# Four weight tiles per run of products in layer 3, and layer 2's scales computed one residual later, in a four-layer graph network on one core

## The chip, the cores and the metric

The kernel runs on one core of a Trainium2 chip. The metric is the device time of one execution in microseconds (us). Before the change it was 2642.23 us, the median of three runs (2640.15 to 2648.64). The profiled execution, from which every duration below comes, took 2647.62 us; its span in the trace is 2645.6 us.

## The reference, cut to what matters

Sixteen graphs of N = 1024 nodes with D = 256 features go through four layers. Each layer adds its result to the stream `x`:

```python
h = jnp.maximum(_layernorm(x), 0.0); x = x + L0(h, adj)   # attention, softmax over the column
h = jnp.maximum(_layernorm(x), 0.0); x = x + L1(h, adj)   # attention, softmax over the row
h = jnp.maximum(_layernorm(x), 0.0); x = x + L2(h, adj)   # mean over the neighbours, relu
h = jnp.maximum(_layernorm(x), 0.0); x = x + L3(h, adj)   # attention with 4 heads of 64, norm per head
```

What the change touches is two steps. Layer 3's attended sum is `einsum('bhij,bhje->bhie', attention, h)` for each of four heads. Layer 2's mean divides by the number of neighbours, `deg`; the kernel folds `deg` into the scale of the layer norm ahead of layer 2, and that scale needs the standard deviation of rows that layer 1 has just written.

## The kernel before, in words

**Tiling.** A graph's nodes are NT = 8 tiles of 128. A "weight tile" `p` is 128 x 1024: 128 neighbours j against all 1024 nodes i. VectorE makes each with one instruction (L920 in layer 3, L812 in layer 1, L759 and L761 in layer 0), and TensorE takes 128-column pieces of it as stationary operand. In layers 0 and 1 a product is 128x128 against 256 or 257 columns (L749, L805) and a graph has 64 of them. In layer 3 there are 4 heads x 8 tiles = 32 weight tiles a graph, and each is used for 8 pieces of nodes, each piece cut in two halves of 64 columns so that the two halves lie in different columns of the array (L930): 16 products a tile, 512 a graph. Every fp32 product leaves two records in the trace, so a weight tile of layer 3 is 32 records.

**Runs.** Layer 3 gives out its weight tiles in runs of `run`: `run` instructions L920 first, and then all their products as one block. `run` is 2, and 1 for the last graph. In a block the last tile's two first pieces stand first (one for each of the two accumulators), then the earlier tiles, then the rest of the last. So a block begins when its last tile is there, and the first tile of a block is released after 4 + 16 of the block's products. The tiles come from a ring of five buffers (tag `p3`, L919): a sixth tile waits until the first has been used. The two accumulators of a head (`ps_o3`, L915) are emptied by ScalarE at the head's end (L938, twice), and the next head's products use the same two.

**The order of the work.** Each graph is a generator that yields a planned time after each piece; L1037 to L1045 always advance the one with the earliest due time. Graphs start 120 units apart while one takes about twice that, so layers 0 and 1 of one graph lie among layers 2, 3 and the tail of the one before. A scheduler then sets the order on each engine from these priorities and its own estimate of readiness; only what is wrapped in `later` keeps program order. [...]

**The norm ahead of layer 2.** `residual` (L719) is called for each node tile i: VectorE adds e and v to x (L726, L727), and after every odd i calls `Norm.pair`: VectorE makes the shifts (L638), ScalarE squares two tiles for their variances (L643). After i = 3 and i = 7, `stds` has GpSimd make the inverse deviations of four tiles (L592, then the power L593). In the norm ahead of layer 2 alone (`times` is given), `stds` then has VectorE make the scales at once (L621, L622), which wait for GpSimd; then `pair` has ScalarE make the normalised tiles hn (L659) for two pairs, TensorE transpose them (`flip`, L672) and ScalarE copy them out (L673).

**Layer 1's sums** are in a ring of two accumulators (`at_ps`): the products of tile i + 2 wait until ScalarE has read those of tile i twice (L828, L830), and these wait for a reciprocal on VectorE (L826).

**Also concerned:** the tail of the graph before (L953 to L990: VectorE, with two squares on ScalarE, L964, whose results use the ring of five too), and the masks of the graph after (L575 on ScalarE, each fed by a load L566).

Of the kernel before, what the change touches and what calls it, by code (L numbers as in the profile page):

```python
# [11 lines left out]
OP = mybir.AluOpType  # L12
# [409 lines left out]
def tile_simple_stack(  # L422
# [11 lines left out]
    nc = tc.nc  # L434
    B, N, D = x.shape
    NT = N // P
# [111 lines left out]
    class Mask:  # L548
# [4 lines left out]
        def __init__(self, b):  # L553
            self.b, self.next, self.raws = b, 0, []
            self.bytes = None
            for _ in range(self.AHEAD):
                self.load()
# [38 lines left out]
    def new_ht():  # L596
        return state.tile([P, DC, N], F32, tag="ht", name="ht", bufs=2)

    class Norm:
# [4 lines left out]


        def __init__(self, times=None):
            self.ht, self.rs, self.waiting, self.times = new_ht(), [], None, times
            if times is not None:
                self.shifts = small.tile([P, NT], F32, tag="shifts", name="shifts", bufs=2)
                self.scales = small.tile([P, 2, NT], F32, tag="scales", name="scales", bufs=2)  # L610
            self.mv = small.tile([P, NT, 2], F32, tag="mv", name="mv", bufs=4)
            self.mean, self.var = self.mv[:, :, 0], self.mv[:, :, 1]

        def stds(self, n, scale):

            k = len(self.rs)
            rs = inv_std(self.var[:, k : k + n], n, scale, 1e-5)
            self.rs += [rs[:, i : i + 1] for i in range(n)]
            if self.times is not None:
                part = slice(k, k + n)  # L620
                nc.vector.tensor_tensor(self.scales[:, 0, part], rs[:, :n], self.times[:, part], op=OP.mult)  # L621
                nc.vector.tensor_tensor(self.scales[:, 1, part], self.scales[:, 0, part], self.shifts[:, part], op=OP.mult)  # L622

        def pair(self, xs, g, sums=None):

            if self.times is None:
                self.flip()
                shift = small.tile([P, 2], F32, tag="shift", name="shift")
            else:
                shift = self.shifts[:, 2 * g : 2 * g + 2]  # L630
            if sums is None:
                for k in range(2 * g, 2 * g + 2):
                    st = small.tile([P, 6], F32, tag="bn", name="st")
                    nc.vector.bn_stats(st, xs[:, k, :])
                    nc.vector.bn_aggr(self.mv[:, k, :], st)
                nc.vector.tensor_scalar(shift, self.mean[:, 2 * g : 2 * g + 2], -1.0, None, op0=OP.mult)
            else:
                nc.vector.tensor_scalar(shift, sums, -1.0 / D, None, op0=OP.mult)  # L638
            if self.times is None:
                self.shifted(xs, g, [(1.0, shift[:, k : k + 1]) for k in range(2)])  # L640
            if sums is not None:
                for k in range(2):
                    nc.scalar.activation(  # L643
                        unread, xs[:, 2 * g + k, :], AF.Square, bias=shift[:, k : k + 1], accum_out=self.var[:, 2 * g + k : 2 * g + k + 1]
                    )
            if sums is None and g == NT // 2 - 1:
                self.stds(NT, 1.0)
            elif sums is not None and g % 2:
                self.stds(NT // 2, 1.0 / D)
                if self.times is not None:  # L650
                    for gg in (g - 1, g):
                        self.flip()
                        self.shifted(xs, gg, [[self.scales[:, k, n : n + 1] for k in range(2)] for n in (2 * gg, 2 * gg + 1)])

        def shifted(self, xs, g, by):
            hns = []
# [24 lines left out]
    def new_hs(name="hs"):  # L681
        return state.tile([P, NT, W3], F32, tag="hs", name=name, bufs=3)
# [36 lines left out]
    def residual(xs, i, v, after, e=None):  # L719

        x = xs[:, i, :]
        if i % 2 == 0:
            after.flip()
            after.sums = small.tile([P, 2], F32, tag="sums", name="sums")
        if e is not None:
            nc.vector.scalar_tensor_tensor(x, e, 1.0, x, op0=OP.min, op1=OP.add)  # L726
        nc.vector.scalar_tensor_tensor(x, v, 0.0, x, op0=OP.max, op1=OP.add, accum_out=after.sums[:, i % 2 : i % 2 + 1])  # L727
        if i % 2:
            after.pair(xs, i // 2, after.sums)
# [159 lines left out]
    def layer3(b, xs, mask, norm, res):  # L889
        hs = new_hs()  # L890
        terms = hs[:, :, D:]
        run = 2 if b < B - 1 else 1
        hb = new_hs("hb")
        hbv = hb[:, :, : H * HW].rearrange("p t (h e) -> p t h e", e=HW)
        for n in range(NT):
            ps = project(norm, wx[3], n, W3)
            nc.scalar.activation(hs[:, n, :], ps[:, :W3], AF.Copy, scale=norm.rs[n])
            if n % 2:
                pair = slice(n - 1, n + 1)
                nc.scalar.activation(hbv[:, pair, :, HO], terms[:, pair, H:], AF.Exp, scale=S3)  # L900
                t = hbv[:, pair, :, :HO]
                hv = hs[:, pair, :D].rearrange("p t (h e) -> p t h e", e=HO)
                bias = rows["bias3"].rearrange("p (h e) -> p h e", e=HO).unsqueeze(1).to_broadcast([P, 2, H, HO])
                nc.vector.tensor_tensor(t, hv, bias, op=OP.add)
                nc.vector.tensor_tensor(t, t, hbv[:, pair, :, HO:].to_broadcast([P, 2, H, HO]), op=OP.mult)
            yield 1.15
        d_row = spread(column(terms[:, :, :H], H), H, (S3 - 1.0,), "l3")
        row = everywhere(d_row[0], "row3")
        watch(b, 2, terms)
        q = small.tile([P, NT, H], F32, tag="q3", name="q3", bufs=2)  # L910
        nc.scalar.activation(q, terms[:, :, H:], AF.Exp, scale=1.0 - S3)
        yield 9.44
        for h in range(H):
            next_row = everywhere(d_row[h + 1], "row3") if h + 1 < H else None
            pss = [hd_ps.tile([P, HALF], F32, tag="hd", name="ps_o3") for _ in range(NHALF)]  # L915
            for j in range(0, NT, run):
                ps_ = []
                for jj in range(j, j + run):
                    p = work.tile([P, N], F32, tag="p3", name="p3", bufs=5)  # L919
                    nc.vector.scalar_tensor_tensor(p, row, q[:, jj, h : h + 1], mask[:, jj, :], op0=OP.max, op1=OP.mult)  # L920
                    ps_.append(p)


                last = run - 1
                runs = [(last, 0), (last, PER)] + [(t, i) for t in range(run) for i in range(NT) if t < last or i % PER]
                for t, i in runs:
                    g, k = divmod(i, PER)
                    for c in range(2):
                        part = slice(c * P // 2, (c + 1) * P // 2)
                        nc.tensor.matmul(  # L930
                            pss[g][part, k * HW : (k + 1) * HW], ps_[t][:, i * P : (i + 1) * P][:, part], hbv[:, j + t, h, :],
                            start=(j == 0 and t == last and k == 0), stop=(j == NT - run and t == last and k == PER - 1),
                            skip_group_check=True,
                        )
                yield 1.4 * run
            for g in range(NHALF):
                o = pss[g][:, : PER * HW].rearrange("p (k e) -> p k e", e=HW)
                nc.scalar.activation(res[:, g * PER : (g + 1) * PER, h, :], o, AF.Relu)  # L938
            row = next_row
        return hs  # L940
# [53 lines left out]
    def graph(b):  # L994
        xs = loaded.pop(b)
        m = masks.pop(b)
        norm = Norm()
        for g in range(NT // 2):
            norm.pair(xs, g)
            m.step()  # L1000
            yield 2.66
        for layer, inputs in ((layer0, (m,)), (layer1, (m.bytes,)), (layer2, ())):
            yield 2.36
            norm.flip()
            after = Norm(degrees(b) if layer is layer1 else None)
            yield from layer(b, xs, *inputs, norm, after)
            norm = after
        yield 1.44
        norm.flip()
        res = state.tile([P, NT, H, HW], F32, tag="res", name="res", bufs=1)  # L1010
        hs = yield from layer3(b, xs, m.bytes, norm, res)
        return tail(b, xs, hs, res)
# [25 lines left out]
    while queue:  # L1038
        queue.sort(key=lambda g: g[:2])
        at, b, g = queue.pop(0)  # L1040
# [86 lines left out]
```

## Time and profile before

| | value |
|---|---|
| time, median of 3 (range) | 2642.23 us (2640.15 to 2648.64) |
| span of the profiled execution | 2645.6 us |
| busy TensorE / VectorE / ScalarE / GpSimd | 2470.5 / 1969.1 / 1449.8 / 378.7 us |
| granted TensorE clock, mean | 0.984 |
| one graph to the next (start of layer 3's products, graphs 1 to 15) | 156.9 to 161.5 us |
| first to last product of layer 3 in one graph | 57.95 us in most graphs |

A line of the timeline gives the start in us, the length, engine and source line, the tiles written and read, and the count of merged records; in square brackets stands how long the engine had been idle and what ended it. A line of the groups gives busy time and mean ns, then the idle time of the engine just before the group. The table of stretches gives each engine's busy time in a stretch.

### The profile page before, as it was taken

What the parts mean: (1) busy time and instruction counts of PE and PEld (TensorE: products, weight loads), DVE (VectorE), ACT (ScalarE), POOL (GpSimd) and SP (SyncE); (2) the same over time, 40 slices, a digit from 0 to 9 for tenths busy, and PEclk for the clock granted to TensorE, in tenths of its full rate; (3) what the DMA queues carried; (4) which work ended last, traced back from release to release, by engine and by line L of the source; (5) the groups of instructions that cost most, each with busy time, mean ns of one, the idle gap of its engine ahead of it and who ended that gap; (6) DMA issues with size and microseconds to landing.
All of it is one profiled execution on the core that took longest, in us unless ns stands there. A gap on an engine that the chain in (4) does not pass through costs nothing.

```text
span 2645.6 us, 62817 instructions
## 1 busy us (share of the span) xinstructions
PE 2470.5 (93%) x26194; PEld 2096.2 (79%) x26194; DVE 1969.1 (74%) x3813; ACT 1449.8 (55%) x4065; POOL 378.7 (14%) x390
## 2 busy tenths in 40 slices
PE   5899999999999999999999999999999999999985
PEld 4688787887878878787887878878787887878864
DVE  4357777787777877778787777877778787777858
ACT  4564755637555374654737556374754737556350
POOL 1010111102111020111102111020111102111011
PEclk7899999999999999999999999999999999999997
DMA  4431241414215142241414215141241414214021
GB/s 152 115 81 57 91 111 58 124 58 129 72 54 152 58 117 70 66 135 57 124 54 132 69 57 152 61 123 60 81 121 58 124 54 132 69 57 124 26 64 35
DMA packets 146073, 233.75 MB, mean 88 GB/s; under 512 B 9393, under 2 KB 94513, under 8 KB 145777
## 3 DMA queue, kind: packets, MB, share of 16 engines
q1 hardware_dynamic: 74608, 145.73, 17.3%
q0 software_dynamic: 71168, 83.89, 13.0%
q8 instruction: 208, 3.41, 0.5%
q14 instruction: 89, 0.72, 0.1%
HBM read 212.35 MB, written 17.24 MB: 87 GB/s over the span
## 4 chain that ended last, share of the span: by engine, by line
PE 60%; DMA 14%; ACT 10%; DVE 9%; issue 5%; POOL 2%; SPq 0%; DVEq 0%; ACTq 0%; POOLq 0%
PE ps_o L749 14%; PE ps_proj L678 14%; PE ps_o L930 10%; PE ps_o L805 8%; PE ps_o L874 6%; DMA raw<-in_adj_t 5%; PE pt_h L672 4%; DMA adj<-in_adj 4%; DVE p L920 3%; PE ps_o L868 3%; DMA row<-d_row 2%; ACT mask L575 2%; ACT hs L810 2%; ACT unread L643 2%; ACT hn L659 1%
## 5 line engine op out<-in xcount | busy, mean ns | idle before, releaser
L920 DVE SCALAR_TENSOR_TENSOR p<-row,q,mask 128x1024 f32<-128x1024 f32 x512 | 633.5, 1279 | 66.1 <-PE ps_o L930 53.2
L930 PEld LDWEIGHTS ps_o<-hb,p 128*64 128x64 f32 x16384 | 503.9, 138 | 99.9 <-issue 47.5
L930 PE MATMUL ps_o<-hb,p 128*64 128x65 f32 x16384 | 543.1, 224 | 19.8 <-ACT res L938 10.3
L805 PE MATMUL ps_o<-hs,p 128*128 128x257 f32 x2048 | 510.7, 392 | 31.0 <-DVE p L812 17.2
L678 PE MATMUL ps_proj<-wx,ht 128*128 128x258 f32 (+2 forms) x2048 | 515.7, 390 | 3.3 <-ACT hs L736 1.1
L749 PE MATMUL ps_o<-hs,p 128*128 128x256 f32 x2048 | 492.2, 385 | 13.6 <-ACT hs L763 13.3
L805 PEld LDWEIGHTS ps_o<-hs,p 128*128 128x128 f32 x2048 | 370.1, 191 | 96.1 <-ACT v L830 24.5
L749 PEld LDWEIGHTS ps_o<-hs,p 128*128 128x128 f32 x2048 | 380.7, 192 | 65.0 <-ACT hs L763 16.5
L678 PEld LDWEIGHTS ps_proj<-wx,ht 128*128 128x128 f32 x2048 | 361.9, 190 | 80.4 <-ACT rest L861 11.6
L726 DVE SCALAR_TENSOR_TENSOR xs<-e,xs 128x256 f32<-128x256 f32 x256 | 108.4, 424 | 261.0 <-ACT e L781 168.9
L592 POOL TENSOR_SCALAR rs<-mv 128x4 f32<-128x4 f32 (+1 forms) x112 | 44.3, 395 | 1583.2 <-ACT unread L643 1568.0
L659 ACT ACTIVATE hn<-xs,shift 128x256 f32<-128x256 f32 x384 | 177.1, 502 | 126.9 <-DVE shift L638 126.6
L593 POOL TENSOR_TENSOR rs<-rs,neg_half 128x4 f32<-128x4 f32 (+2 forms) x144 | 242.8, 1689 | 10.7
L672 PE MATMUL pt_h<-ident,hn 128*128 128x128 f32 x1024 | 181.1, 284 | 41.8 <-ACT hn L659 40.5
L874 PE MATMUL ps_o<-hi,adj 128*128 128x258 f32 x1024 | 202.9, 322 | 15.9 <-DMA adj<-in_adj 14.7
L938 ACT ACTIVATE res<-ps_o 128x260 f32<-128x260 f32 x128 | 44.4, 380 | 310.9 <-PE ps_o L930 310.9
L575 ACT ACTIVATE mask<-raw 128x512 uint8<-128x512 int32 x256 | 160.2, 627 | 76.5 <-DMA raw<-in_adj_t 75.8
L672 PEld LDWEIGHTS pt_h<-ident,hn 128*128 128x128 f32 x1024 | 121.3, 141 | 102.0 <-ACT hn L659 78.2
L874 PEld LDWEIGHTS ps_o<-hi,adj 128*128 128x128 f32 x1024 | 151.6, 190 | 33.3 <-DMA adj<-in_adj 20.3
L727 DVE SCALAR_TENSOR_TENSOR xs<-v,xs 128x256 f32<-128x256 f32 x384 | 161.2, 423 | 19.6 <-ACT v L830 1.0
L759 DVE SCALAR_TENSOR_TENSOR p<-row,q 128x1024 f32<-128x1024 f32 x128 | 160.2, 1272 | 20.2 <-DMA row<-d_row 20.2
L874 PE MATMUL ps_o<-lo,adj 128*128 128x258 f32 x1024 | 163.7, 293 | 0.0
(108 smaller groups left out, 2902.5 us busy)
## 6 DMA issues: line engine op xcount, KB each, us to landing
raw<-in_adj_t SPq DMA_DIRECT2D x256, 256.0 KB
adj<-in_adj POOLq DMA_DIRECT2D x64, 1024.0 KB, 6.0
row<-d_row SPq DMA_DIRECT2D x112, 512.0 KB
xs<-in_x POOLq DMA_DIRECT2D x32, 512.0 KB, 5.5
out<-xs SPq DMA_DIRECT2D x32, 512.0 KB
wx<-in_w SPq DMA_DIRECT2D x3, 256.0 KB
d_row<-e_row SPq DMA_DIRECT2D x48, 4.0 KB
wts<-in_w_t SPq DMA_DIRECT2D x2, 256.0 KB
```

Of the source, the lines that this page charges most:

```text
L575: nc.scalar.activation(self.bytes[:, n, g * HALF : (g + 1) * HALF], raw, AF.Square, accum_out=squares[:, k : k + 1])
L593: nc.gpsimd.tensor_tensor(rs[:, :n], rs[:, :n], neg_half[:, :n], op=OP.pow)
L659: nc.scalar.activation(hn, xs[:, 2 * g + k, :], AF.Relu, scale=scale, bias=bias)
L672: nc.tensor.transpose(pt[:, c, k * P : (k + 1) * P], hn[:, c * P : (c + 1) * P], ident)
L678: nc.tensor.matmul(ps[:, :width], norm.ht[:, c, n * P : (n + 1) * P], w[:, c, :width], start=(c == 0), stop=(c == DC - 1))
L727: nc.vector.scalar_tensor_tensor(x, v, 0.0, x, op0=OP.max, op1=OP.add, accum_out=after.sums[:, i % 2 : i % 2 + 1])
L749: m = nc.tensor.matmul(ps[:, :D], ps_[j][:, i * P : (i + 1) * P], hs[:, j, :D], start=(j == 0), stop=(j == NT - 1))
L759: nc.vector.scalar_tensor_tensor(p, row_a, q[:, j : j + 1], row_b, op0=OP.mult, op1=OP.max)
L805: nc.tensor.matmul(ps[:, : D + 1], ps_[j][:, i * P : (i + 1) * P], hs[:, j, : D + 1], start=(j == 0), stop=(j == NT - 1))
L874: nc.tensor.matmul(ps[:, : D + 2], adj_n[g][:, i, jj : jj + P], h[:, i, : D + 2], start=False, stop=(h is lo and i == NT - 1), skip_group_ ...
L920: nc.vector.scalar_tensor_tensor(p, row, q[:, jj, h : h + 1], mask[:, jj, :], op0=OP.max, op1=OP.mult)
L930: nc.tensor.matmul(pss[g][part, k * HW : (k + 1) * HW], ps_[t][:, i * P : (i + 1) * P][:, part], hbv[:, j + t, h, :], start=(j == 0 and t ...
```

## The change

First, `run` is 4 instead of 2 for all graphs but the last: four L920, then one block of 64 products. Nothing else in layer 3 is edited; the ring stays at five buffers, and the planned time of a run, `1.4 * run`, grows with it.

Second, in the norm ahead of layer 2 the scales, the hn of two pairs and their transposes are no longer emitted when the deviations are asked for. A record `due` is kept, and a new `settle` emits them at the next odd tile's residual, ahead of its VectorE work (so for tiles 0 to 3 at i = 5), or at the layer's end (for tiles 4 to 7). No instruction is added or removed.

```diff
@@ class Norm, __init__ and stds
-            self.ht, self.rs, self.waiting, self.times = new_ht(), [], None, times
+            self.ht, self.rs, self.power, self.waiting, self.times, self.due = new_ht(), [], [], None, times, None
...
-            if self.times is not None:
-                part = slice(k, k + n)
-                nc.vector.tensor_tensor(self.scales[:, 0, part], rs[:, :n], self.times[:, part], op=OP.mult)
-                nc.vector.tensor_tensor(self.scales[:, 1, part], self.scales[:, 0, part], self.shifts[:, part], op=OP.mult)
+            self.power.append(rs[:, :n])
@@ pair
-                if self.times is not None:
-                    for gg in (g - 1, g):
-                        self.flip()
-                        self.shifted(xs, gg, [[self.scales[:, k, n : n + 1] for k in range(2)] for n in (2 * gg, 2 * gg + 1)])
+                self.due = None if self.times is None else (xs, g)
+
+        def settle(self):
+
+            if self.due is None:
+                return
+            (xs, g), self.due = self.due, None
...
+            nc.vector.tensor_tensor(self.scales[:, 0, part], rs, self.times[:, part], op=OP.mult)
+            nc.vector.tensor_tensor(self.scales[:, 1, part], self.scales[:, 0, part], self.shifts[:, part], op=OP.mult)
+            for gg in (g - 1, g):
+                self.flip()
+                self.shifted(xs, gg, [[self.scales[:, k, n : n + 1] for k in range(2)] for n in (2 * gg, 2 * gg + 1)])
@@ residual
-        if i % 2 == 0:
+        if i % 2:
+            after.settle()
+        else:
             after.flip()
@@ layer3
-        run = 2 if b < B - 1 else 1
+        run = 4 if b < B - 1 else 1
@@ graph
             yield 2.36
+            norm.settle()
             norm.flip()
```

More of the change, by code (lines that the diff above doesn't have):

```diff
@@ L649, in pair @@
                 self.stds(NT // 2, 1.0 / D)
-                if self.times is not None:
-                    for gg in (g - 1, g):
-                        self.flip()
-                        self.shifted(xs, gg, [[self.scales[:, k, n : n + 1] for k in range(2)] for n in (2 * gg, 2 * gg + 1)])
+                self.due = None if self.times is None else (xs, g)
[3 more added lines that the diff above has]
+            (xs, g), self.due = self.due, None
+            part = slice(2 * g - 2, 2 * g + 2)
+            k = (g // 2) * (NT // 2)
+            rs = self.power[g // 2]
+            nc.vector.tensor_tensor(self.scales[:, 0, part], rs, self.times[:, part], op=OP.mult)
[3 more added lines that the diff above has]
+                self.shifted(xs, gg, [[self.scales[:, k, n : n + 1] for k in range(2)] for n in (2 * gg, 2 * gg + 1)])
         def shifted(self, xs, g, by):
```

## The prediction, made before the changed kernel ran

> **What bounds the kernel now.** I read the busy shares first, then the table of stretches for one middle graph, then the timelines of TensorE and VectorE in its stretches.
>
> ```profile
> PE 2470.5 (93%) x26194; PEld 2096.2 (79%) x26194; DVE 1969.1 (74%) x3813; ACT 1449.8 (55%) x4065; POOL 378.7 (14%) x390
> ```
> ```profile
> 1018.90:1042.40 23.50, 23.50 (x439) 20.61 (x438) 19.59 (x22) 8.93 (x25) 2.21 (x2) 1.00 0.08 26
> 1042.40:1077.00 34.60, 33.36 (x690) 28.16 (x689) 32.77 (x54) 11.26 (x32) 0.00 (x0) 1.00 0.16 47
> 1077.00:1111.40 34.40, 30.84 (x152) 24.54 (x149) 20.56 (x45) 28.67 (x75) 11.31 (x10) 1.00 0.20 63
> 1111.40:1177.30 65.90, 65.46 (x366) 56.52 (x364) 49.74 (x116) 41.27 (x126) 9.88 (x12) 1.00 0.57 152
> ```
>
> TensorE (second number) sets the pace, but not alone. In layer 3's second stretch VectorE (fourth) is busy 32.77 of 34.60 us, so there it has no slack. The third stretch, layer 1's end, is where TensorE loses most, 3.6 us, to chains through ScalarE and VectorE. The other two stretches are TensorE's.
>
> ```profile
> 1018.93 2.09 PE L930 MATMUL ps_o<-hb,p 128*64 128x65 f32 x64
> 1020.95 3.72 PE L749 MATMUL ps_o<-hs,p 128*128 128x256 f32 x16
> 1024.60 5.82 PE L930 MATMUL ps_o<-hb,p 128*64 128x65 f32 x192
> 1030.35 0.66 PE L672 MATMUL pt_h<-ident,hn 128*128 128x128 f32 x4
> ...
> 1075.02 2.09 PE L930 MATMUL ps_o<-hb,p 128*64 128x65 f32 x64
> 1077.04 7.20 PE L805 MATMUL ps_o<-hs,p 128*128 128x257 f32 x32
> 1084.40 3.73 PE L805 MATMUL ps_o<-hs,p 128*128 128x257 f32 x16 [0.16 <-ACT v L830]
> 1089.62 2.87 PE L805 MATMUL ps_o<-hs,p 128*128 128x257 f32 x12 [1.48 <-ACT v L830]
> 1093.05 0.93 PE L672 MATMUL pt_h<-ident,hn 128*128 128x128 f32 x4 [0.56 <-ACT hn L659]
> ...
> 1109.02 0.88 PE L672 MATMUL pt_h<-ident,hn 128*128 128x128 f32 x6 [1.29 <-ACT hn L659]
> ```
> ```profile
> 1035.01 2.48 DVE L920 SCALAR_TENSOR_TENSOR p<-row,q,mask 128x1024 f32<-128x1024 f32 x2 [1.34 <-PE ps_o L930]
> ...
> 1091.77 0.16 DVE L621 TENSOR_TENSOR scales<-rs,deg 128x4 f32<-128x4 f32 x1 [1.46 <-POOL rs L593]
> ```
>
> See three things. Layer 3 runs in short blocks between products of another shape. VectorE's lead is bounded by the ring (the wait at 1035.01). And the scales hold VectorE for 1.46 us, 73.7 us over the 32 times.
>
> **What the Trainium skill says.** "TensorEngine Tiling (Array Packing)", Key Properties: changing the tiling mode, not just the tile, drains TensorE. L930 works in 64-column tiles, all else in full ones. The trace agrees. Block of 192 records minus block of 64, start to next start, is 5.75 - 2.02 = 3.73 us, so 29.1 ns a record; the 64 keep 2.02 - 1.86 = 0.16 us over. The 16 records L749 take 3.65 where 16 x 216 ns (their spacing inside a row of them) is 3.46: 0.19 over. One block costs **0.35 us** beside its work. "TensorE: Matmul & The Clock Gate", Architectural detail, says ScalarE's and VectorE's queues are strictly first in, first out; so L727, right behind L621, started only at 1091.85.
>
> **The change, part by part.** The compiled order of both kernels has 241 blocks of L930 before and 181 after, so the runs by four do arise. 60 x 0.35 = **-21 us** if nothing else moved: -1.4 us in each of the 15 graphs with `run` = 4, four blocks fewer in each. No instruction is added, SP's order is unchanged, and GpSimd's differs by one early load. All else is waiting, which I priced by walking the new order through that graph with durations from this trace: a tile costs VectorE 1.195 us start to start (seven L812 take 8.45: 1.28 + 6 x 1.195); a run of four costs TensorE 128 x 29.1 = 3.7 us; a run's first buffer is free 1.43 us after its start (1035.01 less the block's start, 1033.58). Times below drop the thousand.
>
> *Layer 3.* With runs of two and five buffers VectorE may be three tiles ahead of a block; with runs of four it is one ahead until that block frees its first buffer. Run 1 starts at 21.6, run 2 at 26.8, run 3 at 33.85, run 4 at 42.25, with 0.2 us of waits; so far TensorE is ahead of the kernel before (42.36 there for the same work). Then there are few other products to fill in. VectorE gets run 5's second buffer at 42.25 + 1.43 = 43.7 and needs three more tiles: 47.3; TensorE was free at 46.35, so **1.0** is lost. Run 6's second tile waits for run 5's first buffer, 48.85, so its last is there at 52.5 while TensorE is free at 51.2: **1.4**. Then eight L812 stand in one row on VectorE, to 62.0, hidden under run 6 and layer 1's products in pairs (to 65.0). Layer 1's third sum needs the first one's accumulator, read by ScalarE at 65.9: **0.85**. Run 7 starts at 68.3; run 8 would at 73.65, its last tile is there at 74.1: **0.45**. It ends at 77.95, where the kernel before ends at 77.04: new waits of 3.9 us replace 1.5 us (0.9 and 0.6, at the same head start and at the first L812) and eat the 1.4 saved; the two ends differ by **+0.9 us.** Row for L812: its exponential (L695) now stands behind both L938, 2.3 us later; landed 5 us after it in the kernel before, it comes at about 52.2, just ahead of VectorE's 52.45. I take 0 for it; the bounds are 0 and, if the two rows sent together land as slowly as the second did, 1.5.
>
> *Scales later.* VectorE still waits for GpSimd's power at L621 in the first half: now behind the fourth sum's L726, but ahead of the tail's L961, whose square (L964) now stands on ScalarE ahead of the fifth sum's e and v, and these ahead of the first hn. So the first hn comes, counted from the variances' end (89.4): GpSimd 2.57 (as before: 1089.20 to 1091.77), L621 and L961 1.3, L964 1.0, e and v 0.7, hn 0.6, to 95.6. TensorE is there at 93.25: **2.35** lost where it lost 0.95 (0.73 and 0.22, start to start). The second half is better: 15 instead of 11 projections of the next graph stand ahead of its transposes, and the wait of 1.45 shrinks to **0.2**, though L979, L982 and L984 now come before L621. The sixth L805 group waits 0.9 instead of 1.65 for v, since TensorE itself is later and has four transposes more to do first. Other small waits in this stretch are 1.2 against 0.5 before. The common point is the fourth pair L868 of layer 2: from layer 3's end I get 33.35 us. The kernel before has 32.9 to 34.4 in its graphs, mean 33.5. **-0.15 us.**
>
> *Sum.* +0.75 us x 15 graphs = +11 us on the span of 2645.6. The profiled execution lies 5.4 us above the median of the plain runs (2647.62 against 2642.23), inside their range; on the median I get **2653 us**.
>
> **The rivals.**
> *The block cost wins (faster).* Place: runs 4 to 6. If VectorE gets tiles to TensorE in time there, the -1.4 us stay. Price: the waits of 1.0 and 1.4 fall to under 1.2 together; then layer 3 ends 0.3 or more earlier and, with the stretch behind it as walked, a graph gains 0.5 to 1.3 us: -8 to -20, 2628 us taken. It decides at 1.2 us. For: TensorE is busy 93%, VectorE idle 26% of the span. Against: the ring lets VectorE use its idle time only one tile ahead, and the stretch is 95% VectorE already.
> *They cancel.* The layer 1 end is limited by chains of ScalarE and VectorE that don't start with TensorE's last layer 3 product; if those absorb the 0.9, the sum is -0.3 to +0.5 a graph: 2643 us. For: 3.6 us of waits there. Against: VectorE too is 0.65 us later at layer 3's end, and its tail starts with L938.
> *The chain behind the scales is longer (slower still).* Masks stand ahead of e, v and the squares on ScalarE, and their loads took 2.9 to 4.4 us in this graph; at the long end the first hn is 1 us later, +1.75 a graph: 2668 us.
> That the runs don't arise is ruled out by the compiled order; only run 6 is cut, by five pairs of L805.
>
> **How the numbers follow.** Forecast, +4 to +20 us: 0.36. Longer chain, +20 to +36: 0.14. Cancel, within 0.3% (8 us, about what can be told from no change): 0.26. Block cost wins: 0.24. The lower part of the forecast's case, up to +8, counts as same: 0.05. So slower 0.45, same 0.31, faster 0.24. The range 2630 to 2670 leaves out some 2 in 10; the forecast's own range is 2646 to 2662.
>
> **What would show it.** Right: 181 blocks; runs 5 and 6 of a head pair starting on "DVE p" with 1 us or more idle; layer 3 lasting 58.5 to 59.5 us where it was 57.95; more than 53.2 us of waits of L920 for L930; the first scaled hn's transposes waiting about 2 us, the second half's nearly none. Wrong: layer 3 shorter than 57.6 us, or no waits for "DVE p" at runs 5 and 6; the forecast of the second stretch falls if L621's wait isn't followed by one of L672.

## The result, and the profile after

The changed kernel takes **2676.03 us** (median of four runs, 2673.54 to 2679.88) where the kernel before takes 2642.64 (2640.15 to 2648.64): ratio **1.0124**, 95% interval 1.0102 to 1.0147. It is slower by 33 us, where the forecast was 11 us slower and the range ended at 2670. The profiled execution has a span of 2678.1 us, 32.5 more than before.

In what follows the lines of the edited code have moved: L920 is now L930, L930 is L940, L938 is L948, L805 is L815, L812 is L822, L672 is L680, L678 is L686, L621 is L657, L874 is L884, L964 is L974. First the busy shares, and the table of stretches for two stretches of a middle graph (from the fourth of layer 3's eight blocks to its last product, then to the common point in layer 2):

```profile
PE 2459.5 (92%) x26194; PEld 2093.9 (78%) x26194; DVE 1964.7 (73%) x3813; ACT 1437.7 (54%) x4065; POOL 383.5 (14%) x390
```
```profile
1212.20:1248.10 35.90, 32.77 (x690) 28.25 (x689) 32.96 (x54) 12.32 (x35) 0.00 (x0) 1.00 0.13 39
1248.10:1281.60 33.50, 30.34 (x154) 24.51 (x149) 21.89 (x47) 27.59 (x73) 11.84 (x10) 1.00 0.23 71
```

TensorE is busy 11 us less than before, which fits the blocks that fell away, and yet the span is longer: its idle time rose from 175 to 219 us. The first stretch does the same 690 products as before in 35.90 us instead of 34.60, and now neither engine is full: TensorE misses 3.1 us and VectorE 2.9 of it. They wait for each other in turn. For the fifth run onwards, TensorE's timeline of the kernel before, then TensorE's and VectorE's of the changed one, show where:

```profile
1044.58 2.09 PE L930 MATMUL ps_o<-hb,p 128*64 128x65 f32 x64
1047.36 4.65 PE L930 MATMUL ps_o<-hb,p 128*64 128x65 f32 x150 [0.69 <-ACT res L938]
1052.56 1.14 PE L805 MATMUL ps_o<-hs,p 128*128 128x257 f32 x4 [0.56 <-DVE p L812]
```
```profile
1212.21 3.95 PE L940 MATMUL ps_o<-hb,p 128*64 128x65 f32 x128
1216.09 0.27 PE L699 MATMUL ps_col<-ident,col 128*8 128x128 f32 x1
1217.46 3.95 PE L940 MATMUL ps_o<-hb,p 128*64 128x65 f32 x128 [1.10 <-ACT e_row L703]
1222.62 1.61 PE L940 MATMUL ps_o<-hb,p 128*64 128x65 f32 x46 [1.20 <-DVE p L930]
...
1236.34 2.43 PE L815 MATMUL ps_o<-hs,p 128*128 128x257 f32 x10 [0.70 <-ACT v L840]
...
1260.43 3.73 PE L815 MATMUL ps_o<-hs,p 128*128 128x257 f32 x16 [1.16 <-ACT v L840]
1265.36 0.87 PE L680 MATMUL pt_h<-ident,hn 128*128 128x128 f32 x6 [1.20 <-ACT hn L667]
```
```profile
1213.64 4.87 DVE L930 SCALAR_TENSOR_TENSOR p<-row,q,mask 128x1024 f32<-128x1024 f32 x4 [0.57 <-PE ps_o L940]
1218.89 3.67 DVE L930 SCALAR_TENSOR_TENSOR p<-row,q,mask 128x1024 f32<-128x1024 f32 x3 [0.37 <-PE ps_o L940]
...
1261.71 0.16 DVE L657 TENSOR_TENSOR scales<-rs,deg 128x4 f32<-128x4 f32 x1 [1.65 <-POOL rs L593]
```

Read the last two fences across. The fourth block starts at 1212.21; 1.43 us later, at 1213.64, VectorE gets its first buffer and starts the last three tiles of the fifth run. They are done 3.67 us later (two steps of 1.195 and a last tile of 1.28), at 1217.31, and at 1217.46 the fifth block starts. (The bracket names L703, a ScalarE instruction; a wait for several things is put down to one of them, and the times show that it was the tile.) The same again: 1217.46, 1218.89, 1222.56, 1222.62. This is a loop: 1.43 + 3.67 + about 0.1 us, measured 5.25 and 5.16 us from block to block, in which TensorE has 3.9 us of work. In the kernel before, the blocks of this stretch follow each other with one wait of 0.69 us, until layer 1's products come in at 1052.56.

The list of waits, TensorE's own rows (total us, times, longest), first of the kernel before, then of the changed one:

```profile
PE pt_h L672 <- ACT hn L659: 40.5, 41, 1.6
...
PE ps_o L874 <- DMA adj<-in_adj: 14.7, 14, 2.6
PE ps_o L805 <- ACT v L830: 13.8, 16, 1.8
...
PE ps_o L930 <- ACT res L938: 10.3, 15, 0.7
PE ps_o L930 <- DVE p L920: 6.4, 1, 6.4
```
```profile
PE pt_h L680 <- ACT hn L667: 39.0, 39, 1.7
PE ps_o L815 <- ACT v L840: 31.4, 30, 1.9
PE ps_o L940 <- DVE p L930: 25.6, 26, 6.1
PE ps_o L884 <- DMA adj<-in_adj: 19.2, 14, 3.0
PE ps_o L940 <- ACT e_row L703: 16.5, 15, 1.1
```

Waits at layer 3's products for a tile (the third row and, as just said, the fifth) went from 6.4 to 42.1 us, while the 10.3 us of waits for L938 to empty an accumulator are gone; so all waits there rose from 18.5 to 42.1. Those of layer 1's products for v went from 13.8 to 31.4, and 0.70 us a graph of it is new at layer 1's third sum, inside layer 3's stage (the line at 1236.34). Those for hn hardly moved.

The stages, worked out from the start times of TensorE's records as means over the 13 middle graphs (the cut points have the same products between them in the first three kernels of the table):

| us per graph | layer 2's stage, to the column of layer 3 | layer 3, to its last product | from there to the fourth pair of layer 2 | sum |
|---|---|---|---|---|
| before | 57.27 | 68.03 | 33.51 | 158.81 |
| changed | 58.16 (+0.89) | 69.52 (+1.49) | 33.83 (+0.32) | 161.51 (+2.70) |
| later scales alone (below) | 57.58 | 67.85 | 32.78 | 158.21 (-0.60) |
| changed, tiles in turn (below) | 56.66 | 67.47 | 33.41 | 157.54 (-1.27) |

15 x 2.70 = 40 us. At the first graph's common point the changed kernel is 6.3 us earlier (3.7 of it by 83 us, most of that in a stretch where TensorE's clock was lower in the trace before), which leaves 34; 32.5 were seen. (In the last row three products of layer 1, six records, have moved from the second stage to the third, so only its sum compares.)

### The profile page after: what moved, and what is told of

Its sections match the earlier page's. It is cut to its first block, busy times and chain, and to the rows that moved or that the text cites. A ratio compares the mean times of both kernels' runs of the same rounds, so it can differ in the third digit from the quotient of the medians.

```text
span 2678.1 us, 62755 instructions
## 1 busy us (share of the span) xinstructions
PE 2459.5 (92%) x26194; PEld 2093.9 (78%) x26194; DVE 1964.7 (73%) x3813; ACT 1437.7 (54%) x4065; POOL 383.5 (14%) x390
## 4 chain that ended last, share of the span: by engine, by line
PE 46%; ACT 18%; DVE 15%; DMA 13%; issue 5%; POOL 2%; SPq 0%; DVEq 0%; ACTq 0%; POOLq 0%
PE ps_o L759 11%; PE ps_proj L686 11%; DVE p L930 8%; PE ps_o L815 7%; PE ps_o L940 7%; PE ps_o L884 6%; DMA adj<-in_adj 4%; ACT hn L667 4%; DMA raw<-in_adj_t 4%; ACT unread L640 3%; DMA row<-d_row 2%; ACT ht L681 2%; ACT hs L820 2%; PE pt_h L680 2%; PE ps_o L878 2%
## 5 line engine op out<-in xcount | busy, mean ns | idle before, releaser
L930 DVE SCALAR_TENSOR_TENSOR p<-row,q,mask 128x1024 f32<-128x1024 f32 x512 | 632.1, 1278 | 58.8 <-PE ps_o L940 48.7
L940 PEld LDWEIGHTS ps_o<-hb,p 128*64 128x64 f32 x16384 | 500.7, 138 | 111.3 <-DVE p L930 51.0
L940 PE MATMUL ps_o<-hb,p 128*64 128x65 f32 x16384 | 530.8, 224 | 46.2 <-DVE p L930 25.6
L815 PE MATMUL ps_o<-hs,p 128*128 128x257 f32 x2048 | 499.8, 389 | 41.9 <-ACT v L840 31.4
L686 PE MATMUL ps_proj<-wx,ht 128*128 128x258 f32 (+2 forms) x2048 | 515.7, 390 | 8.8 <-ACT hs L746 4.4
L759 PE MATMUL ps_o<-hs,p 128*128 128x256 f32 x2048 | 495.2, 386 | 13.8 <-ACT hs L773 13.4
L815 PEld LDWEIGHTS ps_o<-hs,p 128*128 128x128 f32 x2048 | 372.5, 191 | 106.0 <-ACT v L840 43.5
L686 PEld LDWEIGHTS ps_proj<-wx,ht 128*128 128x128 f32 x2048 | 364.5, 191 | 87.0 <-ACT rest L871 12.9
L592 POOL TENSOR_SCALAR rs<-mv 128x4 f32<-128x4 f32 (+1 forms) x112 | 38.4, 343 | 1612.4 <-ACT unread L640 1597.8
L593 POOL TENSOR_TENSOR rs<-rs,neg_half 128x4 f32<-128x4 f32 (+2 forms) x144 | 253.4, 1763 | 10.7
L884 PE MATMUL ps_o<-hi,adj 128*128 128x258 f32 x1024 | 202.3, 322 | 20.1 <-DMA adj<-in_adj 19.2
L680 PE MATMUL pt_h<-ident,hn 128*128 128x128 f32 x1024 | 182.9, 283 | 39.3 <-ACT hn L667 39.0
L680 PEld LDWEIGHTS pt_h<-ident,hn 128*128 128x128 f32 x1024 | 119.7, 141 | 104.4 <-ACT hn L667 85.0
L948 ACT ACTIVATE res<-ps_o 128x260 f32<-128x260 f32 x128 | 44.5, 377 | 275.3 <-PE ps_o L940 275.3
L884 PEld LDWEIGHTS ps_o<-hi,adj 128*128 128x128 f32 x1024 | 152.1, 192 | 39.3 <-DMA adj<-in_adj 24.8
L884 PE MATMUL ps_o<-lo,adj 128*128 128x258 f32 x1024 | 164.0, 294 | 0.0
```

Source lines behind the costliest of these rows:

```text
L593: nc.gpsimd.tensor_tensor(rs[:, :n], rs[:, :n], neg_half[:, :n], op=OP.pow)
L680: nc.tensor.transpose(pt[:, c, k * P : (k + 1) * P], hn[:, c * P : (c + 1) * P], ident)
L686: nc.tensor.matmul(ps[:, :width], norm.ht[:, c, n * P : (n + 1) * P], w[:, c, :width], start=(c == 0), stop=(c == DC - 1))
L759: m = nc.tensor.matmul(ps[:, :D], ps_[j][:, i * P : (i + 1) * P], hs[:, j, :D], start=(j == 0), stop=(j == NT - 1))
L815: nc.tensor.matmul(ps[:, : D + 1], ps_[j][:, i * P : (i + 1) * P], hs[:, j, : D + 1], start=(j == 0), stop=(j == NT - 1))
L884: nc.tensor.matmul(ps[:, : D + 2], adj_n[g][:, i, jj : jj + P], h[:, i, : D + 2], start=False, stop=(h is lo and i == NT - 1), skip_group_ ...
```

## The experiments

The theory at the start: with runs of four and the last tile's products first, the ring of five lets VectorE be only one tile ahead, and that wait costs more than the blocks save. Rivals: the later scales cost the time; or a longer run costs it by itself, whatever the ring.

**Each part alone.** First runs of four with the scales as before, then the later scales with runs of two:

```diff
-        run = 2 if b < B - 1 else 1
+        run = 4 if b < B - 1 else 1
```

> Runs of four tiles, the scales as in the kernel before. Theory lead (a run of four with a ring of five leaves VectorE one tile ahead; its waits, 4.0 us a graph measured against 1.5, outweigh the four blocks of products saved): the waits of 1.2, 1.4 and 0.9 us at runs 5, 6 and the third sum of layer 1 stand as in the changed kernel, layer 3's stage stays 1.5 us longer a graph, and the time is 2663 to 2673 us (+20 to +30). Rival scales (the loss comes from the later scales, in layer 1's end and layer 2): the time is 2640 to 2652.

Measured: 2710.64 us where before is 2648.47, ratio 1.0235 [1.0218, 1.0252]. That is over twice the loss which the theory gave it, so the loop isn't all that a run of four costs. (Every ratio in the experiments is to the kernel before, timed beside it.)

```diff
-        run = 4 if b < B - 1 else 1
+        run = 2 if b < B - 1 else 1
```

> Runs of two tiles, the scales one residual later. Theory lead: 2640 to 2652 us; layer 3's stage is 68.0 us as in the kernel before, and the stretch from layer 3's end to the fourth pair of layer 2's update products changes by under 0.5 us from 33.5. Rival scales: 2660 us or more, with that stretch or layer 2's stage at least 1 us longer a graph.

Measured: 2639.63 us, ratio 0.9969 [0.9959, 0.9979]. So the scales aren't the cost: alone they make the kernel 0.3% faster, and they take back nearly half of what the runs cost. TensorE's waits in the two, runs of four first:

```profile
PE ps_o L805 <- ACT v L830: 37.8, 41, 2.3
PE pt_h L672 <- ACT hn L659: 32.3, 38, 1.7
PE ps_o L930 <- DVE p L920: 26.4, 31, 6.0
PE ps_o L930 <- ACT e_row L695: 16.5, 15, 1.1
```
```profile
PE ps_o L940 <- DVE p L930: 6.0, 1, 6.0
PE ps_o L815 <- ACT v L840: 5.1, 8, 1.2
```

The waits for tiles belong to the runs of four alone (42.9 us against 6.0, which is a single wait). The waits for v are longer with runs of four too, and the later scales shorten them. Where the rest of the 62 us lies is taken up behind the last experiment.

**The ring, with runs of two.** If the lead through the ring is what counts, a smaller ring must hurt the kernel before in the same way, although its blocks don't change or even become fewer. The size is changed at the four places of the tag `p3`:

```diff
-                    p = work.tile([P, N], F32, tag="p3", name="p3", bufs=5)
+                    p = work.tile([P, N], F32, tag="p3", name="p3", bufs=4)
```

> The kernel before with a ring of four tiles instead of five, so that VectorE may be two tiles ahead of a block of two instead of three; the blocks are as many as before, 241. Theory lead: a little of the loss appears, +3 to +15 us. Rival: the lead is worth nothing while VectorE is idle 26% of the span: within 4 us of before.

Measured: 2672.80 us, ratio 1.0094 [1.0077, 1.0110], with 241 blocks as before.

> The kernel before with a ring of three tiles: VectorE is one tile ahead of a block, as in the changed kernel, while a block is only two tiles. 211 blocks instead of 241 in the compiled order. Theory lead: slower by 15 to 45 us, with waits of L930 for L920 as in the changed kernel (before: 28.7 us in all). Rival: within 6 us of before or faster by the 30 blocks fewer (30 x 0.35 = 10 us).

Measured: 2735.92 us, ratio 1.0332 [1.0303, 1.0362], with only 211 blocks: at 0.35 us each they would have saved 10 us. Both cost more than expected. With a ring of three and runs of two VectorE is again one tile ahead, and the timelines of that kernel, TensorE and then VectorE, show the same loop with smaller steps:

```profile
1240.62 2.09 PE L930 MATMUL ps_o<-hb,p 128*64 128x65 f32 x64 [0.48 <-DVE p L920]
1243.49 2.09 PE L930 MATMUL ps_o<-hb,p 128*64 128x65 f32 x64 [0.78 <-DVE p L920]
1246.25 2.09 PE L930 MATMUL ps_o<-hb,p 128*64 128x65 f32 x64 [0.68 <-DVE p L920]
```
```profile
1242.06 2.48 DVE L920 SCALAR_TENSOR_TENSOR p<-row,q,mask 128x1024 f32<-128x1024 f32 x2 [0.29 <-PE ps_o L930]
1244.91 2.48 DVE L920 SCALAR_TENSOR_TENSOR p<-row,q,mask 128x1024 f32<-128x1024 f32 x2 [0.38 <-PE ps_o L930]
```

1240.62 plus 1.44 is 1242.06: the release takes the same time as with runs of four.

**A sixth buffer for the changed kernel.** To make room for it, both kernels of this pair share alterations, which the expectations name; the second is the control.

```diff
-                    p = work.tile([P, N], F32, tag="p3", name="p3", bufs=5)
+                    p = work.tile([P, N], F32, tag="p3", name="p3", bufs=6)
```

> The changed kernel with a ring of six tiles. To make room, layer 1 uses layer 0's weights, and layer 3's bias and the gain of its norm use layer 2's bias row, so that layers 1 and 3 are computed with other numbers; no step of the repeated work is left out, only their loads at the start. 196 blocks instead of 181. Theory lead: VectorE may be two tiles ahead of a run; the waits at runs 5 and 6 (1.2 and 1.4 us) fall by about one tile, 1.2 us, each, and the time by 15 to 35 us against the same kernel with a ring of five, whatever the 15 blocks more cost (5 us). Rival (the loss lies in the length of the last block, which VectorE's and ScalarE's work behind layer 3 waits for): within 8 us of it.

> The changed kernel with a ring of five, as it stands, but with the weights and rows of the run with six (layer 1 with layer 0's weights, layer 3's bias and gain from layer 2's bias row): the control for that run. Both theories: 2660 to 2680 us, at most 10 us less than the changed kernel, since only loads and small steps of the start are gone.

Measured: ring of six 2652.29 us, ratio 1.0018 [1.0006, 1.0030]; control 2671.15 us, ratio 1.0079 [1.0060, 1.0098]. One buffer is worth 19 us. The waits of TensorE's weight loads for tiles, ring of six and then control (one line further down in these kernels):

```profile
PEld ps_o L941 <- DVE p L931: 22.0, 46, 6.4
```
```profile
PEld ps_o L941 <- DVE p L931: 50.4, 75, 6.2
```

The control also shows that the alterations alone are worth some 0.4% against the changed kernel, so the pair is compared within itself.

**The order of the products in a run.** The ring of five is kept, and a block takes its tiles in the order in which they are made, so it can begin with the first tile and gives the first buffer back earlier:

```diff
-                runs = [(last, 0), (last, PER)] + [(t, i) for t in range(run) for i in range(NT) if t < last or i % PER]
+                runs = [(t, i) for t in range(run) for i in range(NT)]
...
-                            start=(j == 0 and t == last and k == 0), stop=(j == NT - run and t == last and k == PER - 1),
+                            start=(j == 0 and t == 0 and k == 0), stop=(j == NT - run and t == last and k == PER - 1),
```

> The changed kernel with a block's products in the order of its tiles: the first tile's 16 first, the last tile's last, so that a block may begin with its first tile and end 0.95 us after its last instead of 3.7. 241 blocks in the compiled order, since the scheduler puts other products between the tiles. Theory lead: the waits at runs 5 and 6 mostly go (the first tile of a run is there one tile after the ring frees it), and the time is 2640 to 2660 us though 60 blocks more cost 21 us. Rival (the runs by four cost through something else, such as their length on TensorE): 2675 us or more, by those blocks.

Measured: 2630.74 us, ratio **0.9926 [0.9909, 0.9944]**, better than forecast. This version beats both kernels. It has 241 blocks, like the kernel before, since the compiled order puts other products between the tiles of a run: here the number of blocks explains nothing. In its trace, TensorE and then VectorE around the fifth and sixth run of another graph:

```profile
1353.72 6.40 PE L940 MATMUL ps_o<-hb,p 128*64 128x65 f32 x210 [0.68 <-ACT res L948]
1360.64 1.13 PE L815 MATMUL ps_o<-hs,p 128*128 128x257 f32 x4 [0.53 <-DVE p L822]
```
```profile
1350.08 8.51 DVE L930 SCALAR_TENSOR_TENSOR p<-row,q,mask 128x1024 f32<-128x1024 f32 x7 [0.34 <-PE ps_o L940]
1359.30 9.65 DVE L822 SCALAR_TENSOR_TENSOR p<-row,q,mask 128x1024 f32<-128x1024 f32 x8 [0.70 <-DMA row<-d_row]
```

VectorE makes seven tiles without a pause where the changed kernel paused after four, and TensorE takes 210 records in one go. What ends last now is another wait: VectorE's first L822 waits for its row from a DMA, and TensorE for that tile. TensorE's waits in this version:

```profile
PE ps_o L815 <- DVE p L822: 20.6, 16, 7.5
...
PE ps_o L940 <- DVE p L930: 6.1, 1, 6.1
...
PE ps_o L815 <- ACT v L840: 0.9, 2, 0.7
```

The same order with runs of two:

> Runs of two, the scales one residual later, and a block's products in the order of its tiles. 271 blocks instead of 241. Theory lead: with runs of two VectorE is three tiles ahead already and layer 3 waits only 1.5 us a graph, so the order of tiles wins at most 1 us a graph and the 30 blocks cost 0.7: within 12 us of the run with runs of two and later scales alone (2640). Rival: TensorE waits tile by tile and the time grows by 20 us or more.

Measured: 2637.35 us, ratio 0.9946 [0.9928, 0.9965]. Against the last tile first, the turn lowers the ratio by 0.0023 with runs of two (0.9969 to 0.9946, intervals that overlap) and by 0.0198 with runs of four (1.0124 to 0.9926). So the length of the run isn't bad in itself: in turn, four is 7 us faster than two in the medians, though the two intervals overlap.

**In turn without the later scales, and with a sixth buffer.** The first of the three is the kernel with runs of four alone, and the order above; the other two are the pair with rings of six and five, and the order above.

> Runs of four with the tiles taken in turn, as in the changed kernel in turn, but layer 2's scales as in the kernel before; 241 blocks. Runs of four alone, last tile first, cost 61 us, and with the later scales only 33. Theory A (the run's own waits are the cost, and the scales act beside them): the turn takes those waits away whatever the scales do; from the runs of two in turn to the runs of four in turn the time fell by 6.6 us, and the later scales alone were worth 8.2, so this kernel is 2635 to 2645 where before is 2649 (ratio 0.995 to 0.9985). Theory B (with runs of four the scales' chain of GpSimd's power itself gets longer, which the later scales hide): 20 to 30 us more than the version with later scales, 2651 to 2661 (ratio 1.001 to 1.0045).

Measured: 2657.16 us where before is now 2656.35, ratio 1.0004 [0.9995, 1.0012]. That lies between the two forecasts. The turn takes the waits for tiles away here too; but the later scales are worth 0.8% with runs of four in turn (1.0004 to 0.9926) where they are worth 0.3% with runs of two. The two parts of the change do act on each other.

> The changed kernel with its tiles in turn and a ring of six; as in the two runs before with these rows, layer 1 uses layer 0's weights, and layer 3's bias and gain rows are those of layer 2's bias. If VectorE's lead was what runs of four lacked, taking the tiles in turn has given most of it back, and the sixth buffer is now worth 0 to 9 us against its own control (it was worth 19 with the last tile first). If the ring limits as before, it is worth 15 to 25 us.

> Control for the ring of six in turn: ring of five, the same alterations, tiles in turn. The alterations alone took the changed kernel from 1.0124 to 1.0079 of the kernel before, so here about 0.9926 - 0.0045 = 0.988 (2618 us where before is 2649); if the alterations only moved waits of the long runs, no gain: 0.9926 (2630).

Measured: 2637.44 us, ratio 0.9927 [0.9910, 0.9945], with six buffers, and 2628.35 us, 0.9907 [0.9887, 0.9927], with five. In turn the sixth buffer isn't worth anything (the kernel with it is 9 us slower in the medians, with intervals that overlap); with the last tile first it was worth 19 us. That speaks for one cause behind both remedies: a further buffer lets VectorE be further ahead, the turn lets a block begin with fewer of its tiles, and once one of them has been done, the other gives nothing.

**Where the parts lie.** The table of stages above can't take in runs of four alone, whose update products of layer 2 stand elsewhere. Cut one update product later, at the fifth pair, the first six kernels below have the same products in each stage, and the last two agree with each other (against the six, three products of layer 1 have moved from layer 3's stage to the next):

| us per graph | layer 2's stage | layer 3 | from there to the fifth pair of layer 2 | sum |
|---|---|---|---|---|
| before | 44.64 | 68.03 | 46.14 | 158.81 |
| runs of four alone | 44.72 | 69.87 (+1.84) | 48.74 (+2.60) | 163.32 (+4.52) |
| changed | 45.30 (+0.66) | 69.52 (+1.49) | 46.69 (+0.55) | 161.51 (+2.70) |
| later scales alone | 44.69 | 67.85 (-0.18) | 45.61 (-0.53) | 158.16 (-0.65) |
| before, ring of four | 44.52 | 69.21 (+1.18) | 46.20 (+0.06) | 159.93 (+1.12) |
| before, ring of three | 44.59 | 71.47 (+3.44) | 48.85 (+2.71) | 164.91 (+6.10) |
| in turn, runs of four alone | 44.46 | 67.30 | 47.03 | 158.79 |
| in turn, changed | 44.63 | 67.47 | 45.42 | 157.52 |

So layer 3 loses 1.5 to 1.8 us a graph to runs of four, whatever the scales do; that is where the loop stands. Runs of four alone lose more than that, 2.60 us, behind layer 3, at layer 1's end, and that is what the later scales take back: 2.05 us a graph there with runs of four, 1.61 in turn, 0.53 with runs of two. Times 15 graphs these are 31, 24 and 8 us, close to the 29, 21 and 8 us by which the ratios differ. Which of the chains at layer 1's end makes those 2.60 us isn't settled: no run moved one of them alone. (A ring of three costs 2.71 us there too. The squares L964 use the same ring, and their part in it wasn't separated.)

## Why the prediction was wrong, point by point

The side was right, the size wrong by 23 us. The mechanism named, VectorE one tile ahead of a block, is the one that the runs show in layer 3. What failed is the *Sum*, +0.75 us a graph where +2.70 were measured, and each of its terms: layer 3 (+0.9, measured +1.49), the stretch with the later scales (-0.15, measured +0.32), and layer 2's stage, put at nothing without a reason (measured +0.89).

**Two bases in one sum, and luck with the side.** Layer 3's +0.9 is a difference within the graph walked, whose layer 3 was short (67.2 us, mean 68.03). The -0.15 is a difference from the mean, 33.5, while the stretch 1077.0 to 1111.4 of the graph walked is long, 34.4. Within that one graph the forecast 33.35 means -1.05, and the sum is -0.15 us a graph: no change. Against the means on both sides, 68.1 and 33.35 give about -0.1. Nor do the waits listed for the later scales lead to 33.35: +1.4, -1.25, -0.75 and +0.7 make +0.1. So that the forecast said "slower" came in part from joining a short layer 3 to a mean stretch.

**The block cost holds.** There are 181 blocks. By the medians of start-to-start times, entering the 64-column tiles costs 93 ns over a usual spacing (310 against 217), leaving them 123 (152 against 29), and the first product after that another 104 (321 against 217): 0.32 us where 0.35 was taken. By this price 60 blocks fewer are worth 19 us. (TensorE's busy time fell by 11; it also holds short stalls and stretches at half clock, so it doesn't measure the blocks alone.)

**The walk through layer 3** had the right waits. Times after the transposed column of layer 3, measured in the graph shown above, the one after the graph walked:

| us | run 1 | 2 | 3 | 4 | 5 | 6 | 7 | 8 | end |
|---|---|---|---|---|---|---|---|---|---|
| predicted | 11.75 | 16.95 | 24.0 | 32.4 | 37.5 | 42.7 | 58.45 | 64.25 | 68.1 |
| measured | 11.98 | 17.15 | 24.89 | 33.35 | 38.61 | 43.76 | 59.85 | 65.43 | 69.3 |

The waits of 1.0 and 1.4 at runs 5 and 6 were 1.17 and 1.42 (starts, against a usual spacing), the 0.85 at layer 1's third sum was 0.86; run 8 waited less than the 0.45 given. Two terms were too small. Between runs 2 and 3 0.7 us are missing: the twelve records of projections there take 3.2 us instead of 12 x 0.2165 = 2.6, and one waits for ScalarE, which now has two L948 of the head before ahead of the copy of the transposes. I had walked TensorE and VectorE, and ScalarE only where the change moved a row. And between runs 6 and 7, in the run cut by layer 1's pairs, 0.3. So the end came at 69.3 instead of 68.1. Against the graph walked (67.2) that is +2.1; the graphs of the kernel before take 67.0 to 68.8, and on the means layer 3 costs **+1.5, where +0.9 was forecast**. Row for L812, taken at 0, cost nothing in this graph; VectorE goes from the last L930 to L822 without a pause.

**Scales later.** In the graph shown, the first scaled hn's transposes wait 1.36 us, not 2.35, the second half's 0.95, not 0.2; together 2.3 instead of 2.55. Still the stretch got longer, **+0.32 instead of -0.15**. What was put at 0.9, a group L805's wait for v, is 1.16 in the graph shown and 0.8 to 1.85 in the 13 middle graphs, with a mean of 1.4. What the walk left out is that the other half of the change moves this stretch too. With the later scales and runs of two it is 32.78, with runs of four 33.83. ScalarE's timeline, changed kernel first (its last layer 3 product is at 1248.0), then later scales alone (1229.8):

```profile
1253.67 0.47 ACT L840 ACTIVATE v<-ps_o,shares 128x256 f32<-128x256 f32 x1
...
1256.12 0.63 ACT L575 ACTIVATE mask<-raw 128x512 uint8<-128x512 int32 x1 [0.65 <-DMA raw<-in_adj_t]
1256.65 0.19 ACT L575 ACTIVATION_READ_ACCUMULATOR mask<-raw 128x1 f32 x1
1256.75 1.04 ACT L974 ACTIVATE sq<-res 128x1024 f32<-128x1024 f32 x1
```
```profile
1235.73 0.47 ACT L840 ACTIVATE v<-ps_o,shares 128x256 f32<-128x256 f32 x1
...
1236.88 0.63 ACT L575 ACTIVATE mask<-raw 128x512 uint8<-128x512 int32 x1
1237.41 0.19 ACT L575 ACTIVATION_READ_ACCUMULATOR mask<-raw 128x1 f32 x1
1237.52 1.06 ACT L974 ACTIVATE sq<-res 128x1024 f32<-128x1024 f32 x1
```

In the changed kernel three masks stand between v and the square, not two, and the third waits for its load: the square starts 8.75 us after layer 3's last product instead of 7.7. What stands behind it on ScalarE is later too, and through VectorE's sums so is TensorE's work: e, v, the first scaled hn. The Trainium skill's page "TensorE: Matmul & The Clock Gate", Architectural detail, on strictly ordered queues, is borne out once more: L657's wait of 1.65 at 1261.71 also holds the L971 for the second square, which starts at 1261.79. That masks would stand ahead of the squares was in the rival with the longer chain (+1.75 a graph), with a chance of 0.14; its place was right, its hn not. The lengthening by about 1 us is shown by the stages of the two kernels; that the third mask is its cause is read from two graphs, and no run moved the mask alone.

**Layer 2's stage** was put at nothing, and took **+0.89**. Most of it lies in four of the 13 graphs. In these TensorE waited 1.9 to 3.0 us for the adjacency, and its granted clock was then halved for 3.4 us, which costs 1.7 us of work. One of the four, and the whole stage around it:

```profile
1303.29 0.87 PE L884 MATMUL ps_o<-hi,adj 128*128 128x258 f32 x5 [1.90 <-DMA adj<-in_adj]
```
```profile
1304.40:1307.80 3.40, 3.40 (x11) 2.76 (x11) 3.40 (x11) 0.51 (x1) 0.00 (x0) 0.50 1.30 242
1281.50:1350.80 69.30, 67.16 (x369) 58.16 (x368) 48.35 (x113) 41.85 (x128) 9.79 (x12) 0.98 0.54 145
```

In the kernel before this happened in one of the 13 graphs. Without these graphs the stage takes 57.28 us against 57.03, and cut at the fifth pair 44.46 against 44.39. So about 0.6 of the 0.89 are such waits with the slow clock behind them, and the remaining 0.25 lies between the fourth and the fifth pair. Whether the change brings the waits about stays open: in the trace of runs of four alone the clock is never halved in this stage, and each kernel has one trace.

**The markers.** Runs 5 and 6 waiting over 1 us: seen. "More than 53.2 us of waits of L920": wrong, 48.7; VectorE waits less often (45 times for 60), and what lengthens the time is TensorE's waiting for it. "Layer 3 lasting 58.5 to 59.5": first to last product is 57.2 us in most graphs although the stage got longer, because the first block now starts after six more products of layer 0 (2.7 us). The marker measured from a point that the change moves; by its letter the sign of being wrong, "shorter than 57.6 us", came true while the waits that it was to tell of were there.

**The rivals.** "The block cost wins" needed the waits at runs 5 and 6 to be under 1.2 us together; they are 2.6. The kernel does become faster when the tiles are taken in turn, but not by this rival's means: there the blocks are as many as before. "They cancel" fell with the rise outside layer 3: nothing there absorbed the delay. The longer chain came nearest, 2668, and masks ahead of the squares are a part of what was seen; but it put the whole excess over the forecast there, while most of it lies in layer 3 and in layer 2's stage, so the nearness of its number is partly luck. What also stays open: which chain behind layer 3 the later scales shorten so much more with runs of four than with runs of two (2.05 us a graph against 0.53). The waits for v follow it (37.8 to 31.4, 13.8 to 5.1 in the fences above), but only in part.

## What to carry to other kernels

When a producer and a consumer share a ring, count how many tiles the producer can be ahead at the moment a block starts: ring minus run, here 1. With a lead of one and the last tile needed first, a block then takes at least the release plus run - 1 tiles of the producer (here 1.43 + 3.67 us, against 3.9 us of products), however much idle time the producer has on average. Before paying for it with another buffer, let the consumer take the tiles in the order in which they are made; and when the change moves an order that a scheduler makes, walk the third engine's queue too. Take every term of a sum against the same base, the same graph or the mean of all. Look at the granted clock of each stretch before looking for a cause.

## What the runs showed of the hardware that was not expected

The release of a buffer is steady: in the changed kernel all 45 of VectorE's waits for it ended 1.42 to 1.44 us after the block's start, and the median is 1.43 with runs of two as well. The 40 records ahead of it take 40 x 29.1 ns = 1.16 us; so some 0.27 us pass between the start of the last reading record and the writer's start, as the traces show too (median 0.27). And a single buffer in a ring moved the whole kernel by 0.9% (five to four, runs of two) and a further 2.4% (four to three), while six instead of five gave 0.7% or nothing depending on the order of the products alone. A wait of TensorE far shorter than a stage can also cost more than itself: in each of the four graphs named above the granted clock fell to 0.50 for 3.4 us, 2.2 to 3.0 us after a wait of 1.9 to 3.0 us had begun. Not every such wait brought this: in another graph of the same trace a wait of 2.08 us left the clock at 1.00.
